# Layer 3 of a convolution network on one core: where the gate's product stands among the mask products

## The chip, the core and the metric

The kernel runs on one core of a Trainium2 chip. The metric is device time of one launch in microseconds. The five engines run their own instruction streams and meet at semaphores: PE (TensorE, the matmuls; its weight loads are shown as PEld), DVE (VectorE), ACT (ScalarE), POOL (GpSimd) and SP (SyncE); POOL and SP issue the transfers here. PE writes into PSUM, [...]and DVE and ACT read it from there.

## The reference, cut to what matters

Four layers, each a group norm and a convolution block with a residual, on x of 4 images, 48 channels, 256 x 256 pixels, all fp32. The change is in the last one:

```
y = einsum('oc,bchw->bohw', w_in, gn(x))              # 48 -> 288 channels
f = rfft2(y in 8x8 patches) * fft_mask                # one mask per channel
y = depthwise_conv3x3(irfft2(f))                      # across patch borders
x1, x2 = split(y, 2, axis=1)
out = x + einsum('oc,bchw->bohw', w_out, gelu(x1) * x2)
```

## The kernel before, in words

Layers 0 to 2 come first (about the first 11,240 us); layer 3 runs from there to the end. Its 288 channels are done in two passes of 144, the first from about 11,310 to 13,858 us and the second to 15,960 us. A pass has 64 jobs (4 images by 16 row blocks of 16 rows); a job is a row block in patches of 8 x 8, held as 64 Fourier coefficients per patch. The 128 jobs are software-pipelined in `layer3`: one turn of its last loop is a "step", and in step s the stages work on different jobs:

- `stage_a`, `stage_b` (pass 1 only) turn the normalised input of the next job into its spectrum xf and store it; in pass 2 `load_xf` (L1201, SP) reads it back in four pieces.
- `stage_c`, called as c(0) to c(7), for the current job: 8 matmuls (16 records, L1216) multiply the spectrum by w_in into the PSUM tile py, of which there is one (two banks); then four DVE products with the mask (L1228, "mask products", a pair for v=0 and a pair for v=1) write z in SBUF. c(i+1) overwrites py, so its first matmul waits for all four.
- `edges` e1 and e0 compute the border pixels of the patches (L1253), ACT copies them (L1254), and SP stores them to HBM (L1257); `above_below` and `sides` read neighbours' borders back into rows 64 to 99 of z with POOL transfers (L1266 to L1272).
- `stage_v`, called as v(0) to v(11), for the job two steps back: v(i) is half t = i % 2 of channel group g = i // 2. 12 matmuls (24 records, L1288) do inverse transform and 3x3 convolution at once into pg. An even v is followed by a gelu on ACT (L1299, into gall), an odd v by the gate's product on DVE (L1301, gall times pg). pg of even and of odd v are one bank each, with a single buffer: v(5) cannot start before the product of v(3) has read its bank, nor v(11) before that of v(9).
- `stage_t`, `last_out`, `add_out` for the job three steps back: transposes (L1309), the output matmuls (L1334), the addition to xo on DVE (L1347) and the store on SP (L1350); `load_out` (L1323, POOL) loads xo.

The order of work is written out by hand at the end of the loop and kept as it stands, engine by engine. The part in question, one step's second half:

```
            c(4), e0(0), e0(1), e0(2)
            if jv:
                load_out(jv)
            if jb:
                above_below(jb, 1)
            a(1), v(2), norm(2)
            c(5), v(3), b(1), v(4, 5)
            c(6), v(6), a(2), v(7), norm(3), v(8)
            c(7), v(9), b(2), v(10), a(3), v(11), norm(4)
```

On PE, c(5) is followed by v(3), v(4), v(5) in pass 2, where a() and the matmuls of b() are absent. In the next step come c(0), e1, the transposes, c(1), the output matmuls, c(2), more transposes, and then v(0), v(1): the first that need the border rows of z that `above_below(jb, 1)` loaded.

Of the kernel before, what the change touches and what calls it, by code (L numbers as in the profile page):

```python
# [1090 lines left out]
def layer3(k):  # L1091
# [11 lines left out]
    with ExitStack() as ctx:  # L1103
# [48 lines left out]
        def load_x(j, st):  # L1152

            for hf in range(2):
                r0 = j.u * RU + 8 * st
                nc.sync.dma_start(
                    xin[st][hf * HP : hf * HP + C], k.x3[j.b][:, r0 : r0 + 8, hf * 128 : (hf + 1) * 128]
                )

        def normalise(j, q):  # L1160
            xn = sp.tile([P112, 8, 8, 8], F32, name="xn")
            nc.scalar.activation(
                xn.rearrange("p k r w -> p r k w"),
                xin[q // 2][:, :, q % 2 * 64 : q % 2 * 64 + 64].rearrange("p r (k w) -> p r k w", w=8),
                AF.Identity,
                bias=ab3[:, j.b, 1:2],
                scale=ab3[:, j.b, 0:1],
            )
            j.x = xn.rearrange("p (k v) r w -> p k (v r w)", v=2)

        def stage_a(j):

            pt = bank()
            for i in range(4):
                nc.tensor.transpose(pt[:, i * P112 : (i + 1) * P112], j.x[:, i, :], k.ident[:P112, :P112])
            j.xt = sp.tile([128, 4, P112], F32, name="xt")
            nc.scalar.copy(j.xt.rearrange("p i c -> p (i c)"), pt[:, : 4 * P112])
# [25 lines left out]
        def columns(z):  # L1203

            return z[:, 2 : 2 + 2 * ZW].rearrange("p (s c n e) -> p s c n e", s=2, n=ZS, e=2)

        def stage_c(j, ci):

            py = ps_c.tile([128, 2, 512], F32, name="py")
            xf = j.xf[ci // 2]  # L1210
            for ii in range(2):
                i = 2 * (ci % 2) + ii
                for v in range(2):
                    for hf in range(2):
                        p = slice(hf * HP, hf * HP + C)
                        nc.tensor.matmul(  # L1216
                            py[v * HP : (v + 1) * HP, hf, ii * PASS : (ii + 1) * PASS],
                            xf[p, i, v, :],
                            wi[p, j.ps, :],
                            start=True,  # L1220
                            stop=True,
                        )
            for v in range(2):
                p = slice(v * HP, v * HP + HP)
                for hf in range(2):
                    n = hf * NPC // 2 + 4 * (ci % 4)
                    out = columns(j.z[0:64])[:, ci // 4, :, n : n + 4].rearrange("p c (i v) e -> p c i v e", v=2)
                    nc.vector.tensor_tensor(  # L1228
                        out[:, :, :, v, :],
                        py[p, hf, : 2 * PASS].rearrange("p (i c e) -> p c i e", i=2, e=2),  # L1230
                        meff[p, j.ps].rearrange("p (c e) -> p c e", e=2)[:, :, None, :].broadcast_to(
                            [HP, PASS // 2, 2, 2]
                        ),
                        ALU.mult,
                    )

# [38 lines left out]
        def load_k(j, g):  # L1277
            t = k.k3[g] = kp.tile([KZ, 4 * GP, 64], F32, name=f"kw{g}")
            nc.sync.dma_start(t.rearrange("p j x -> p (j x)"), k.kw[j.ps, g])

        def stage_v(j, g, t):


            z = columns(j.z)[..., :NPC, :]
            pg = ps_g.tile([128, GP, 2, NPC], F32, name=f"pg{t}", padded_shape=[128, 8, 2, NPC])
            for kk in range(GP):
                for e in range(2):
                    nc.tensor.matmul(  # L1288
                        pg[e * HP : (e + 1) * HP, kk],
                        k.k3[g][:, (t * GP + kk) * 2 + e, :],  # L1290
                        z[:, :, t * NP2 + g * GP + kk, :, e],
                        start=True,
                        stop=True,
                    )
            o = gall[:, g * GP : (g + 1) * GP]
            o = bass.AP(tensor=o.tensor, offset=o.offset, ap=[o.ap[0], [HP * NPC, 2], [NPC, GP], [1, NPC]])
            pg = pg.rearrange("p k s n -> p s k n")
            if t == 0:
                nc.scalar.activation(o, pg, AF.Gelu)  # L1299
            else:  # L1300
                nc.vector.tensor_tensor(o, o, pg, ALU.mult)  # L1301

        def stage_t(j, q):

            pt = [bank() for e in range(2)]
            for m in range(8):
                for e in range(2):
                    p = slice(e * HP, (e + 1) * HP)
                    nc.tensor.transpose(  # L1309
                        pt[e][: HP + NP2, m * 64 : (m + 1) * 64], gall[p, :, 8 * q + m], k.ident[p, p]  # L1310
                    )
            j.gt[q] = sp.tile([HP + NP2, 2, 512], F32, name="gt", bufs=2)
            for e in range(2):
                nc.scalar.copy(j.gt[q][:, e], pt[e][: HP + NP2])
# [10 lines left out]
        def last_out(j, h):  # L1325

            po = [bank() for st in range(2)]
            for qq in range(2):
                for e in range(2):
                    for cc in range(2):  # L1330
                        for st in range(2):
                            p = slice(st * HP, st * HP + NP2)
                            n = (HP, C)[cc]
                            nc.tensor.matmul(  # L1334
                                po[st][cc * HP : cc * HP + n, qq * 256 : (qq + 1) * 256],
                                wo[p, j.ps, e, :n],
                                j.gt[2 * h + qq][p, e, :].rearrange("p (m q x) -> p q m x", q=2, x=32)[:, cc],
                                start=(e == 0),
                                stop=(e == 1),
                            )  # L1340
            j.po = po
# [33 lines left out]
        for s in range(len(jobs) + 3):  # L1375
            jp, jc, jb, jv, jt = job(s + 1), job(s), job(s - 1), job(s - 2), job(s - 3)
            def a(q):
                if jp and not jp.ps:
                    stage_a(jp)

            def norm(q):

                nxt = jp if q < 4 else job(s + 2)
                if nxt and not nxt.ps:
                    normalise(nxt, q % 4)
                    after = job(nxt.at + 1)
                    if q % 2 and after and not after.ps:
                        load_x(after, q // 2)

            def b(q):  # L1390
                j = jp if q < 3 else jc
                if j:
                    (load_xf if j.ps else stage_b)(j, q)

            def c(i):
                if jc:
                    stage_c(jc, i)

            def t(i):
                if jt:  # L1400
                    stage_t(jt, i)

            def o(q):
                if jt:
                    last_out(jt, q)

            def v(*parts):
                for i in parts if jv else ():
                    stage_v(jv, i // 2, i % 2)
                    nxt = job(jv.at + 1)  # L1410
                    if i % 2 and nxt and nxt.ps != jv.ps:
                        load_k(nxt, i // 2)

            def e1(h):
                if jb:
                    edges(jb, 1, h)

            def e0(h):
                if jc:
                    edges(jc, 0, h)  # L1420

            def add(h):
                if jt:
                    add_out(jt, h)

            if jc:
                jc.z = zs[jc.at % 3]
            c(0), e1(0), t(0), e1(1), t(1), e1(2)
            if jb:
                above_below(jb, 0)  # L1430
                sides(jb)
            c(1), o(0), add(0), b(3)
            c(2), t(2), a(0), t(3), norm(1), v(0, 1)
            c(3), o(1), add(1), b(0)
# [3 lines that stand above are left out]
            if jb:  # L1438
                above_below(jb, 1)
            a(1), v(2), norm(2)  # L1440
            c(5), v(3), b(1), v(4, 5)
            c(6), v(6), a(2), v(7), norm(3), v(8)
            c(7), v(9), b(2), v(10), a(3), v(11), norm(4)

# [3 lines left out]
def network(ctx: ExitStack, tc: tile.TileContext, a):  # L1450
# [36 lines left out]
    layer1(k)  # L1487
    layer2(k)
    layer3(k)


# [150 lines left out]
```

## Time and profile before

| | |
|---|---|
| median of three runs | 16065.99 us (16065.2 to 16119.82) |
| the profiled execution: its time / its span | 16076.35 us / 16074.6 us |
| mean granted TensorE clock in it | 0.929 |
| mask products, L1228 | 4096 of 450 ns |
| gate's products, L1301 | 768 of 554 ns |
| gate matmuls, L1288 | 36864 records, 217 to 370 ns |
| gelus, L1299 | 768 of 492 ns |

The page's first part gives each engine's busy time; its second part cuts the span into 40 slices of 402 us, in which layer 3 has the last twelve. "PEclk" is the TensorE clock that was granted, in tenths of full speed. In the list of waits a row such as "PE pg L1288 <- DVE gall L1301" says that PE stood idle before a matmul of line 1288 until DVE finished an instruction of line 1301; the numbers are the sum in us, how often, and the longest. "issue" is idle time for which the profile shows no wait. In a timeline, equal instructions in a row are merged: start, length, engine, line, operation, count, and in brackets the idle time before them.

### The profile page before, as it was taken

The numbers are of one execution on the slowest core, as the hardware profiler recorded it, in microseconds if no ns is written. First come the engines' busy times: TensorE is split into PE (matmuls) and PEld (weight loads), VectorE is DVE, ScalarE is ACT, GpSimd is POOL, SyncE is SP. The second block draws the span as 40 slices with busy tenths as digits, with TensorE's granted clock in tenths as the row PEclk, the third lists the DMA queues.
The fourth block names the chain that finished last, engine by engine and source line by source line (L and its number), as shares of the span: only waits on it lengthen the run. The fifth ranks groups of instructions, "written<-read, shape, count | busy, mean of one in ns | idle before, by whom it ended". The sixth has DMA issues, their size and how long they took to land.

```text
span 16074.6 us, 464532 instructions
## 1 busy us (share of the span) xinstructions
PE 14620.7 (91%) x206010; PEld 10189.7 (63%) x206010; DVE 7278.4 (45%) x17024; ACT 5817.9 (36%) x11327; POOL 3452.9 (21%) x3593
## 2 busy tenths in 40 slices
PE   2988898988999999899999999998899999899998
PEld 1888884336676767555555555555666666666666
DVE  4000003333333546566666666665444444555555
ACT  1222221114432310455555555554444444323222
POOL 0000000000000036454545454544111111111111
PEclk9999999999999999999999999999778788888888
DMA  7565558998766689332322222222777777777877
GB/s 181 114 117 112 113 114 125 142 134 131 138 146 142 152 187 228 45 38 34 37 34 37 35 37 35 36 35 32 144 138 148 145 144 145 155 155 156 160 153 147
DMA packets 1998550, 1807.51 MB, mean 112 GB/s; under 512 B 1476444, under 2 KB 1755873, under 8 KB 1959489
## 3 DMA queue, kind: packets, MB, share of 16 engines
q1 hardware_dynamic: 1931002, 1501.81, 48.9%
q0 software_dynamic: 65536, 275.97, 11.0%
q8 instruction: 1617, 26.49, 0.8%
q14 instruction: 395, 3.24, 0.1%
HBM read 967.67 MB, written 625.68 MB: 99 GB/s over the span
## 4 chain that ended last, share of the span: by engine, by line
PE 80%; DMA 6%; DVE 6%; issue 4%; SPq 2%; ACT 1%; POOL 0%; DVEq 0%; POOLq 0%; ACTq 0%
PE pc L817 16%; PE p L468 14%; PE pg L1288 8%; PE ps_qk L277 7%; PE ps_o L369 5%; PE py L1216 4%; PE pm L1253 4%; PE pm L1334 3%; PE pa L848 3%; PE pm L1309 2%; PE pb L873 2%; PE gram L260 2%; PE ps_qk L281 2%; PE pb L918 2%; PE pb L927 2%
## 5 line engine op out<-in xcount | busy, mean ns | idle before, releaser
L817 PE MATMUL pc<-wg,t 50*64 50x288 f32 x49152 | 3374.9, 406 | 151.8 <-DVE qkv L833 112.5
L817 PEld LDWEIGHTS pc<-wg,t 50*64 50x64 f32 x49152 | 2013.2, 133 | 1458.3 <-issue 317.9
L1228 DVE TENSOR_TENSOR z<-py,meff 64x288 f32<-64x288 f32 x4096 | 1686.4, 450 | 1186.0 <-PE py L1216 1162.5
L1288 PE MATMUL pg<-z,kw 100*64 100x64 f32 x36864 | 1599.7, 248 | 227.5 <-issue 121.8
L1288 PEld LDWEIGHTS pg<-z,kw 100*64 100x64 f32 x36864 | 1438.8, 158 | 460.3 <-issue 275.7
L277 PE MATMUL ps_qk<-wa,ta 108*64 108x96 f32 x24576 | 1444.5, 253 | 156.1 <-issue 124.5
L468 PE MATMUL p<-carry,wk_down 96*96 96x256 f32 x6120 | 1353.3, 383 | 94.3 <-DVE carry L473 56.7
L911 POOL TENSOR_TENSOR z<-z,gb 128x768 f32<-128x768 f32 x512 | 933.1, 1822 | 2098.6 <-ACT z L905 1582.1
L277 PEld LDWEIGHTS ps_qk<-wa,ta 108*64 108x64 f32 x24576 | 1222.6, 142 | 197.7 <-issue 181.8
L833 DVE TENSOR_TENSOR qkv<-pc,c 128x576 f32<-128x576 f32 x1024 | 772.5, 754 | 1232.0 <-ACT c L832 1211.1
L468 PEld LDWEIGHTS p<-carry,wk_down 96*96 96x96 f32 x6120 | 1007.6, 165 | 439.6 <-DVE carry L473 70.1
L369 PE MATMUL ps_o<-xn,wc 48*64 48x512 f32 x9216 | 1038.9, 607 | 67.7 <-issue 49.8
L636 POOL TENSOR_TENSOR x1in<-carry,x1in 96x256 f32<-96x256 f32 x512 | 433.7, 854 | 2410.4 <-DMA x1in<-x 2215.5
L1216 PE MATMUL py<-wi,xf 48*64 48x144 f32 x16384 | 875.8, 332 | 67.8 <-issue 37.0
L840 DVE TENSOR_TENSOR qkv<-pc,qkv 128x576 f32<-128x576 f32 x1024 | 773.0, 755 | 338.7 <-PE pc L817 310.3
L1301 DVE TENSOR_TENSOR gall<-gall,pg 128x384 f32<-128x384 f32 x768 | 425.5, 554 | 1067.8 <-PE pg L1288 838.6
L369 PEld LDWEIGHTS ps_o<-xn,wc 48*64 48x64 f32 x9216 | 392.6, 137 | 713.3 <-issue 683.1
L283 ACT COPY qk<-ps_qk 128x384 f32<-128x384 f32 x512 | 244.5, 478 | 1630.2 <-PE ps_qk L281 1630.2
L281 PE MATMUL ps_qk<-wb,tb 108*64 108x96 f32 x8192 | 751.8, 253 | 84.0 <-issue 55.0
L1299 ACT ACTIVATE gall<-pg 128x384 f32<-128x384 f32 x768 | 377.5, 492 | 1043.3 <-PE pg L1288 1040.4
L173 DVE COPY g<-gram 96x96 f32<-96x96 f32 x4 | 1.0, 254 | 1657.1 <-PE gram L260 1657.1
L1216 PEld LDWEIGHTS py<-wi,xf 48*64 48x64 f32 x16384 | 564.3, 152 | 292.2 <-issue 163.9
(161 smaller groups left out, 20931.0 us busy)
## 6 DMA issues: line engine op xcount, KB each, us to landing
eb<-yb SPq DMA_DIRECT2D x1024, 148.5 KB
z<-eb POOLq DMA_DIRECT2D x512, 297.0 KB, 10.4
xf<-xf SPq DMA_DIRECT2D x512, 224.0 KB
tb<-ta SPq DMA_DIRECT2D x192, 576.0 KB
ta<-ta SPq DMA_DIRECT2D x64, 864.0 KB
xr<-x SPq DMA_DIRECT2D x120, 432.0 KB
xt<-in_x SPq DMA_DIRECT2D x32, 1536.0 KB
res<-in_x SPq DMA_DIRECT2D x64, 768.0 KB
```

The lines of the kernel that those rows point to most:

```text
L277: nc.tensor.matmul(o, ta[:, rr + dy, cols], wa[:, dy, :], start=(dy == 0), stop=False)
L281: nc.tensor.matmul(o, tb[:, rr, cols], wb, start=False, stop=True)
L369: nc.tensor.matmul(ps[cp_ * HP : (cp_ + 1) * HP, hf, :], wc[p, t, :], xn[p, r : r + 2, t % 3 : t % 3 + W], start=(t == 0), stop=(t == 8),)
L468: nc.tensor.matmul(pv, wk[name][:, o, :], old[:, :, o : o + N], start=(o == 0), stop=(o == 2))
L817: nc.tensor.matmul(pc[cc * HP : (cc + 1) * HP, h, :O], j.t[p, which, n, w0 : w0 + HP], wg[p, which, dx], start=(dx == 0), stop=(dx == 2),)
L833: nc.vector.tensor_tensor(j.qkv[:, g // 2, :, g % 2], j.pc[1][:, 0:1, :O].broadcast_to([128, 2, O]), c2, ALU.add)
L840: nc.vector.tensor_tensor(o, j.pc[0][:, :, :O], o, ALU.add)
L911: nc.gpsimd.tensor_tensor(z, z, gb[:, i : i + 1, :].broadcast_to([128, 8, Q]), op)
L1216: nc.tensor.matmul(py[v * HP : (v + 1) * HP, hf, ii * PASS : (ii + 1) * PASS], xf[p, i, v, :], wi[p, j.ps, :], start=True, stop=True,)
L1228: nc.vector.tensor_tensor(out[:, :, :, v, :], py[p, hf, : 2 * PASS].rearrange("p (i c e) -> p c i e", i=2, e=2), meff[p, j.ps].rearrange(" ...
L1253: nc.tensor.matmul(pb[32 * q : 32 * q + 32, :n], mb, z[:, a : a + n], start=True, stop=True)
L1288: nc.tensor.matmul(pg[e * HP : (e + 1) * HP, kk], k.k3[g][:, (t * GP + kk) * 2 + e, :], z[:, :, t * NP2 + g * GP + kk, :, e], start=True, ...
```

## The change

The four mask products of `stage_c` become two calls of an inner function `mask(v)`; `stage_c` issues the first and returns the second. `c(i, ...)` issues the v parts that it is given between the two. It is given v(3) with c(5) and v(9) with c(7), which stood right behind them before; all other c have nothing between.

```diff
-            for v in range(2):
+            def mask(v):
                 p = slice(v * HP, v * HP + HP)
                 for hf in range(2):
...
                         ALU.mult,
                     )
+
+            mask(0)
+            return lambda: mask(1)
...
-            def c(i):
-                if jc:
-                    stage_c(jc, i)
+            def c(i, *between):
+
+                rest = stage_c(jc, i) if jc else None
+                v(*between)
+                if rest:
+                    rest()
...
             a(1), v(2), norm(2)
-            c(5), v(3), b(1), v(4, 5)
+            c(5, 3), b(1), v(4, 5)
             c(6), v(6), a(2), v(7), norm(3), v(8)
-            c(7), v(9), b(2), v(10), a(3), v(11), norm(4)
+            c(7, 9), b(2), v(10), a(3), v(11), norm(4)
```

The order on PE, ACT, POOL and SP stays as it was. On DVE, twice a step, mask, mask, mask, mask, product becomes mask, mask, product, mask, mask. In the last turns, where there is no current job, c(5, 3) and c(7, 9) issue their v part alone.

## The prediction

> **What bounds the kernel now.** I read the page first, then the two passes of layer 3 as stretches of their own, then PE's waits in pass 2, then the timeline of a step.
>
> ```profile
> PE 14620.7 (91%) x206010; PEld 10189.7 (63%) x206010; DVE 7278.4 (45%) x17024; ACT 5817.9 (36%) x11327; POOL 3452.9 (21%) x3593
> PEclk9999999999999999999999999999778788888888
> DMA  7565558998766689332322222222777777777877
> ```
>
> PE is the engine that is nearly always busy; DVE is not near its limit. In the last twelve slices, which are layer 3, the granted clock is no longer full and the DMA engines are at 0.7 to 0.8.
>
> ```profile
> PE pg L1288 <- DVE gall L1301: 75.5, 102, 0.8
> PE pg L1288 <- issue: 51.6, 39, 4.3
> PE pg L1288 <- DMA z<-eb: 24.3, 12, 4.9
> PE pm L1309 <- DVE xo L1347: 16.6, 18, 3.7
> ```
>
> These are PE's waits in pass 2 (13,858 to 15,960 us). The first row is what the change aims at: 102 waits of 0.74 us (over the whole trace 78.5 us in 106). The same list for pass 1 has no such row: there the transforms of b(1) and of b(2) and a(3) lie between the product and v(5) or v(11), and cover it. The third row will matter too. One place in the timeline, PE and then DVE:
>
> ```profile
> 14042.82 0.72 PE L1216 MATMUL py<-wi,xf 48*64 48x144 f32 x16
> 14043.48 1.71 PE L1288 MATMUL pg<-z,kw 100*64 100x64 f32 x48
> 14045.92 0.95 PE L1288 MATMUL pg<-z,kw 100*64 100x64 f32 x24 [0.73 <-DVE gall L1301]
> 14046.80 0.46 PE L1216 MATMUL py<-wi,xf 48*64 48x144 f32 x5
> ...
> 14043.61 1.66 DVE L1228 TENSOR_TENSOR z<-py,meff 64x288 f32<-64x288 f32 x4 [1.66 <-PE py L1216]
> 14045.31 0.56 DVE L1301 TENSOR_TENSOR gall<-gall,pg 128x384 f32<-128x384 f32 x1
> 14046.99 0.56 DVE L1301 TENSOR_TENSOR gall<-gall,pg 128x384 f32<-128x384 f32 x1 [1.12 <-PE pg L1288]
> ```
>
> c(5) at 42.82 (I drop the 14,000), v(3) and v(4) from 43.48, v(5) at 45.92, c(6) at 46.80. DVE does four masks to 45.27, then the product of v(3) to 45.87; 0.05 us later v(5) starts.
>
> **The change at one place, full clock, pass 2.** Nothing is added or removed: as many DVE instructions, of the same durations, in another order; no transfer is moved, and no queue but DVE's is reordered. The first pair of masks ends at 43.61 + 1.66/2 = 44.44. The product then waits for PE: where DVE stands free, the product of v(5) starts 46.99 - 45.92 = 1.07 us after that v's first matmul, so that of v(3) starts at 43.48 + 1.07 = 44.55 (DVE idles 0.11 us, with the second mask pair behind it) and ends at 45.11. Its other input, the gelu of v(2), ended at 43.44 and doesn't delay it. v(5) can start at 45.16; v(4)'s matmuls are issued until about 45.0, so the wait all but vanishes: 45.92 - 45.16 = 0.76 us sooner.
>
> What is late next? The second pair ends at 45.13 + 0.83 = 45.96, 0.7 us later than before, and c(6) must wait for it because py is single. c(6) would come at 46.80 - 0.76 = 46.04, py is free at about 46.01. So that cover is just enough; if it fails by a tenth, the price is 0.1 us x 106 = 11 us. Edges don't feel the later masks: z of c(5) and c(7) is first read by e1 of the next step.
>
> So at most 106 x 0.75 = 80 us lie here. At half clock nothing is to be had: the product is released by slower matmuls, and v(5) and v(11) show no wait on it. In pass 1 the second pair also ends 0.7 us later, but c(6) and c(0) come 4.0 us or more after their predecessors at full clock, well behind it; I put pass 1 at nothing (bounds: 4 us gained, where v(5) is barely covered, 5 lost).
>
> **Where the saved time goes.** Both places lie between e0, which starts the chain of border transfers, and v(0) of the next step, which needs them. Here is a step in which v(0) came to wait:
>
> ```profile
> 14943.22 0.57 POOL L1323 DMA_DIRECT2D xo<-y  x1 [10.86 <-DVE z L1228]
> 14948.74 0.51 POOL L1266 DMA_DIRECT2D z<-eb  x1 [4.05 <-DMA eb<-yb]
> 14949.75 0.51 POOL L1268 DMA_DIRECT2D z<-eb  x1
> ...
> 14955.37 1.62 PE L1309 MATMUL pm<-ident,gall 64*100 64x64 f32 x32
> 14959.47 2.83 PE L1288 MATMUL pg<-z,kw 100*64 100x64 f32 x48 [2.48 <-DMA z<-eb]
> ```
>
> The borders are stored by SP, read by POOL at 948.74 to 949.75, and land some 9 us later. PE got there 2.48 us early although it had lost 1.48 us at v(5) and v(11). I compared, job by job in pass 2, the last landing of z<-eb with the first matmul of v(0): in 27 of 60 jobs v(0) starts within 0.55 us of it. From c(4), a full-clock step needs 24.2 us to v(0) without such a wait, and the landing comes after 22 to 28 us, median 25.8. Where the landing is last, PE saves 1.5 us earlier and waits 1.5 us longer at v(0). Summing for each step the smaller of its slack there and its two stalls gives 34.9 of 68.4 us in 58 steps; scaled to the 78.5 us, **40 us**; with the occasional py wait, about 35.
>
> **The clock.** These stretches are a clean step, a step held by the landing but at full clock, and the two steps around the wait of 2.48 us (columns: length, busy time of PE, PEld, DVE, ACT, POOL, granted clock, DMA share, GB/s):
>
> ```profile
> 14345.02:14373.35 28.33, 26.65 (x592) 19.42 (x593) 18.84 (x43) 9.77 (x20) 4.73 (x9) 1.00 0.80 164
> 14535.92:14566.42 30.50, 27.29 (x592) 19.92 (x593) 18.91 (x43) 9.86 (x20) 5.10 (x10) 1.00 0.82 164
> 14932.62:14966.66 34.04, 29.97 (x592) 22.00 (x596) 18.86 (x42) 9.86 (x20) 5.34 (x10) 0.89 0.86 164
> 14966.66:15000.07 33.41, 32.48 (x597) 22.94 (x589) 18.89 (x43) 9.76 (x20) 5.34 (x10) 0.81 0.77 144
> 14959.00:14979.50 20.50, 20.03 (x264) 14.12 (x264) 7.80 (x17) 2.94 (x6) 5.34 (x10) 0.50 0.81 156
> ```
>
> The wait was followed by 20.5 us at half clock. The two steps took 67.45 us against 2 x 30.50 = 61: a price of 6.5 us. Pass 2 has 38 such drops, 519 us at half clock in all. About 15 begin around v(0), mostly for 17 to 24 us, where z or xo is late; waits of z above 2.1 us nearly all brought one, waits about 1 us mostly not. Ten begin within 5 us behind one of the waits that the change removes (106 us at half clock, so some 53 us lost, since a half-clock us costs about half a us), most of them with an "issue" gap as well.
>
> The Trainium skill speaks to this ("TensorE: Matmul & The Clock Gate", section on the HAM clock gate): the clock halves after an idle window of about 3.4 us. By that rule moving 1.5 us into a wait of 1 us costs no clock, and only the 35 us count. By the row above 2.48 us sufficed. The trace decides: I expect more long drops at v(0), about four more at 6.5 us (26 us), and about half of the ten others gone (26 us). These cancel, and neither can be sized better than to a factor of two.
>
> **The sum.** 16076.35 - 35 = 16041 in the profiled execution's own terms; that one was 10 us above the median, so from the median 16066 - 35 = **16031 us**.
>
> **The rivals.**
> - *The gain comes in full, and the clock helps* (chance 0.22). The denser PE stream loses the ten drops: -80 and up to -53 more, net of landings between 15,935 and 15,990, say 15,975. For it: landing times follow e0, which follows PE, so the chain is earlier too in later steps. Against it: 27 of 60 jobs have no slack now.
> - *The wait just moves* (0.20). The DMA share of 0.80 to 0.86 in full-clock steps means the transfers set the pace of every run of fast steps; slack after a slow step is used up sooner. Gain 5 us: 16,060. The same time would follow if the second pair were late for c(6) by as much as the product is early. That the order is not carried out is unlikely: in the timeline above DVE does exactly the written order.
> - *More half clock* (0.14). At v(0) of pass 2, waits of 1 us become 2.5 us, and the clock halves for 20 us at 6.5 us a time. It beats the 35 us from six net added drops on, and needs 18 to be slower by 0.5% (115/6.5). Fourteen steps now wait 0.4 to 1.5 us there without much harm; with twelve more, +43: 16,109. Against it: each drop gives the transfers time to catch up (after one, slack is 9 to 14 us), so drops prevent one another.
>
> The partial gain, 16,031, keeps 0.44. I call "same" what is within 0.5%, or 80 us, about what a measurement of this kernel can tell from no change. Faster (below 15,986) takes most of the first rival and a little of the main case, 0.20; slower (above 16,146) takes the larger part of the last, 0.10; same 0.70. The range goes from the full gain without much of the clock's help, 15,945, to more half clock, 16,115.
>
> **What would show it.** In the changed profile the row "pg <- gall" on PE should fall from 75 us to under 10 in pass 2 (the step of the product); c(6) should come 3.2 us after c(5) in place of 4.0, with little or no wait of py on the masks; waits of v(0) on z<-eb, 24 us now, should double (the step of the landing); half clock in pass 2 should stay near 519 us. If it moves by more than 150 us either way, the clock has decided, and my cancelling was wrong; if the z waits stay as they are, the full gain should be there; pass 1 should keep its 2,548 us.

## The result, and the profile after

The changed kernel takes 16085.24 us (median of 14 runs, 16031.29 to 16119.74) against 16071.19 us of 14 runs of the kernel before. The ratio worked out from all of these runs is 1.0004, 95% interval 0.999 to 1.0017. That is no change that can be measured, and the 35 us of gain that the prediction named as likeliest lie outside the interval. The profiled execution took 16058.56 us, with a span of 16056.8 us. One execution of the seventh experiment below, of 22,851 us, was far slower than all its like and is left out there.

The same three rows of the page, after (the changed kernel's lines have other numbers: L1217 is L1216 of before, L1230 is L1228, L1293 is L1288, L1306 is L1301):

```profile
PE 14671.9 (91%) x206010; PEld 10254.8 (64%) x206010; DVE 7280.5 (45%) x17024; ACT 5819.9 (36%) x11327; POOL 3453.0 (22%) x3593
PEclk9999999999999999999999999999788877888888
DMA  8565658998766679322222222222677777777877
```

PE shows 51 us more busy time for the same 206010 matmuls: they ran at a lower clock (0.925 in the mean, 0.929 before). PE's waits in pass 2, after:

```profile
PE pg L1293 <- issue: 47.4, 41, 3.2
PE pm L1314 <- issue: 18.4, 12, 3.8
PE pg L1293 <- DMA z<-eb: 16.9, 15, 2.3
PE pm L1314 <- DVE xo L1352: 16.6, 21, 2.7
...
PE pg L1293 <- DVE gall L1306: 0.3, 1, 0.3
```

The wait that the change aims at went from 75.5 us to 0.3 us. The waits for the border transfers, which were to double, fell from 24.3 to 16.9 us. The timeline of one place, PE and then DVE (c(5), then v(3) to v(5) in one run, then c(6)):

```profile
14665.10 0.72 PE L1217 MATMUL py<-wi,xf 48*64 48x144 f32 x16
14665.75 2.64 PE L1293 MATMUL pg<-z,kw 100*64 100x64 f32 x72
14668.32 0.72 PE L1217 MATMUL py<-wi,xf 48*64 48x144 f32 x16
...
14665.89 0.81 DVE L1230 TENSOR_TENSOR z<-py,meff 64x288 f32<-64x288 f32 x2 [1.65 <-PE py L1217]
14666.83 0.55 DVE L1306 TENSOR_TENSOR gall<-gall,pg 128x384 f32<-128x384 f32 x1
14667.41 0.84 DVE L1230 TENSOR_TENSOR z<-py,meff 64x288 f32<-64x288 f32 x2
```

c(6) comes 3.22 us after c(5) (3.98 before), and its py is free in time: the second mask pair ends at 68.25, c(6) starts at 68.32. So the place does what was worked out. Here is pass 2 as a whole, from c(0) of its first job to c(0) of its last, before and then after:

```profile
13871.36:15972.28 2100.92, 1898.67 (x37301) 1370.21 (x37297) 1189.93 (x2646) 621.01 (x1260) 337.07 (x631) 0.88 0.79 157
```

```profile
13862.76:15954.27 2091.51, 1948.23 (x37300) 1397.35 (x37297) 1189.67 (x2646) 622.65 (x1260) 338.52 (x633) 0.85 0.79 158
```

The length hardly moved, and the granted clock fell from 0.88 to 0.85. The first two numbers of each row show where the time went: PE's idle time, length less busy time, fell by 59 us (202 to 143), and the same matmuls took 50 us longer (1898.67 to 1948.23). The trace's record of the clock has only full and half: in pass 2, 519 us at half before and 628 us after. If a us at half clock counts as half a us of work, pass 2 is 2100.9 - 259 = 1841 us at full clock before and 2091.5 - 314 = 1777 after: by this estimate 64 us were freed, and 55 given back through the clock. By stretches of a step (from each c to the next, means in us over 60 steps of pass 2, counted from the trace):

| from | c(0) | c(1) | c(2) | c(3) | c(4) | c(5) | c(6) | c(7) |
|---|---|---|---|---|---|---|---|---|
| length before | 5.21 | 3.13 | 5.48 | 2.92 | 4.23 | 4.36 | 3.54 | 4.49 |
| length after | 5.61 | 3.43 | 5.57 | 3.01 | 4.40 | 3.77 | 3.58 | 3.74 |
| at half clock before | 1.05 | 0.80 | 2.15 | 0.86 | 1.23 | 0.98 | 0.64 | 0.48 |
| at half clock after | 1.19 | 1.50 | 2.51 | 1.08 | 1.56 | 1.16 | 0.37 | 0.35 |
| clock drops begun before / after | 2 / 12 | 5 / 7 | 15 / 14 | 0 / 0 | 0 / 0 | 4 / 0 | 2 / 3 | 8 / 4 |

1.34 us a step are gained behind c(5) and c(7), and 1.05 lost from c(0) to c(4). A "drop" is a change from full to half clock; 38 begin in pass 2 before and 43 after. Those behind c(5) to c(7) are halved (14 to 7); ten new ones begin behind c(0).

**What "issue" is.** Waits without a visible cause are 72 us of PE's waits in pass 2 before, against 120 for all others, and 95 us after, against 38. I compared the 46 of them above 0.7 us in pass 2 after (84.9 us; before 38 with 61.8 us) with the DMA packets of the queue of kind "instruction": these are 16,384 bytes each, and 8 in 10 of the waits end 1.31 to 1.95 us after the end of such a packet, where 8 in 10 instants drawn at random lie 0.7 to 8.2 us after one. They stand mostly at multiples of 256 PE instructions, matmuls and weight loads together, from one another. So PE waits for its own code ("late code" below), and it does so less when there is less data to move (the fifth experiment) and more when the transfers are bunched (the third). The Trainium skill ("Runtime: NRT & Kernel Launch", "Instruction fetch mechanics") has the blocks of 16 KiB and calls the cost of going from one to the next mostly hidden; here 85 us aren't. One such wait, PE's timeline and then the stretch behind it (columns as in the prediction):

```profile
14684.17 1.53 PE L1314 MATMUL pm<-ident,gall 64*100 64x64 f32 x30 [0.67 <-issue]
14688.54 2.79 PE L1293 MATMUL pg<-z,kw 100*64 100x64 f32 x48 [2.85 <-issue]
```

```profile
14688.60:14692.10 3.50, 3.50 (x64) 3.38 (x68) 0.56 (x1) 0.49 (x1) 2.25 (x5) 0.51 0.52 100
```

After 2.85 us without code the clock is at half.

### The profile page after: what moved, and what is told of

The parts are those of the page before. It is cut to its first block, busy times and chain, and to the rows that moved or that the text cites. A ratio compares the mean times of both kernels' runs of the same rounds, so it can differ in the third digit from the quotient of the medians.

```text
span 16056.8 us, 464660 instructions
## 1 busy us (share of the span) xinstructions
PE 14671.9 (91%) x206010; PEld 10254.8 (64%) x206010; DVE 7280.5 (45%) x17024; ACT 5819.9 (36%) x11327; POOL 3453.0 (22%) x3593
## 4 chain that ended last, share of the span: by engine, by line
PE 80%; DMA 6%; DVE 6%; issue 5%; SPq 1%; ACT 1%; POOL 0%; DVEq 0%; POOLq 0%; ACTq 0%
PE pc L817 15%; PE p L468 15%; PE pg L1293 9%; PE ps_qk L277 7%; PE ps_o L369 6%; PE py L1217 4%; PE pm L1258 4%; PE pm L1339 3%; PE pa L848 3%; PE gram L260 3%; PE pb L873 2%; PE pm L1314 2%; PE ps_qk L281 2%; PE pb L918 2%; PE pb L927 2%
## 5 line engine op out<-in xcount | busy, mean ns | idle before, releaser
L1230 DVE TENSOR_TENSOR z<-py,meff 64x288 f32<-64x288 f32 x4096 | 1684.9, 450 | 1227.8 <-PE py L1217 1199.3
L1293 PE MATMUL pg<-z,kw 100*64 100x64 f32 x36864 | 1592.0, 248 | 139.7 <-issue 120.0
L1293 PEld LDWEIGHTS pg<-z,kw 100*64 100x64 f32 x36864 | 1433.7, 158 | 369.5 <-issue 260.4
L1217 PE MATMUL py<-wi,xf 48*64 48x144 f32 x16384 | 884.3, 336 | 68.8 <-issue 40.3
L1306 DVE TENSOR_TENSOR gall<-gall,pg 128x384 f32<-128x384 f32 x768 | 425.6, 554 | 970.5 <-PE pg L1293 725.0
L369 PEld LDWEIGHTS ps_o<-xn,wc 48*64 48x64 f32 x9216 | 432.0, 138 | 676.1 <-issue 628.2
L1217 PEld LDWEIGHTS py<-wi,xf 48*64 48x64 f32 x16384 | 572.2, 154 | 297.4 <-issue 175.5
L1258 PE MATMUL pm<-z,mb 64*32 64x396 f32 x6144 | 737.6, 581 | 15.5 <-issue 14.3
```

Source lines behind the costliest of these rows:

```text
L369: nc.tensor.matmul(ps[cp_ * HP : (cp_ + 1) * HP, hf, :], wc[p, t, :], xn[p, r : r + 2, t % 3 : t % 3 + W], start=(t == 0), stop=(t == 8),)
L1217: nc.tensor.matmul(py[v * HP : (v + 1) * HP, hf, ii * PASS : (ii + 1) * PASS], xf[p, i, v, :], wi[p, j.ps, :], start=True, stop=True,)
L1230: nc.vector.tensor_tensor(out[:, :, :, v, :], py[p, hf, : 2 * PASS].rearrange("p (i c e) -> p c i e", i=2, e=2), meff[p, j.ps].rearrange(" ...
L1258: nc.tensor.matmul(pb[32 * q : 32 * q + 32, :n], mb, z[:, a : a + n], start=True, stop=True)
L1293: nc.tensor.matmul(pg[e * HP : (e + 1) * HP, kk], k.k3[g][:, (t * GP + kk) * 2 + e, :], z[:, :, t * NP2 + g * GP + kk, :, e], start=True, ...
```

## The experiments

Each experiment edits either the kernel before ("old order") or the changed one ("new order"), and two kernels that differ by the order alone are twins. Theories. *Clock*: PE's freed time arrives, and more half-clock time takes it back. *Landing*: the border transfers set the step, and the wait moves there. *Load*, a form of the first: late code and late data, both from busy DMA engines, open the gaps that halve the clock. The rivals were that the two places differ, or that a denser PE stream is slowed whatever the transfers do.

**1 and 2. One place at a time.** With c(5) alone:

```diff
-            c(7, 9), b(2), v(10), a(3), v(11), norm(4)
+            c(7), v(9), b(2), v(10), a(3), v(11), norm(4)
```

> The change at c(5) alone, c(7) and v(9) as before. Clock theory (the removed waits of PE arrive in full as time at full clock, and more time at half clock takes them back): PE's wait of the gate matmuls on the gate's product falls from 75 to about 38 us in pass 2, pass 2 less half of its half-clock time falls by some 30 us (from 1841), its half-clock time lies above the 519 us of before, and the time is within 25 us of before. Landing theory (the transfers of borders set the step, whatever the clock): waits of v(0) on them rise by some 15 us and the time stays; half clock unchanged. If the two places act differently: this one alone faster by 30 us or more.

And c(7) alone:

```diff
-            c(5, 3), b(1), v(4, 5)
+            c(5), v(3), b(1), v(4, 5)
```

> The change at c(7) alone, c(5) and v(3) as before. Clock theory: as with the first place alone, wait on the product about 38 us, time within 25 us of before, half clock above 519 us in pass 2. Landing theory: waits of v(0) on the borders up by 15 us, time unchanged, half clock unchanged. If the two places act differently: one of them alone is faster by 30 us and the other slower by as much.

16096.9 and 16095.87 us: ratios to before 1.0013 (1.0002 to 1.0024) and 1.0013 (1.0001 to 1.0025), so if anything a little slower than before. The wait on the product fell to 42.6 and 32.5 us. Pass 2 at full clock, reckoned as above, was 1817 and 1803 us, half clock 577 and 604 us. Half the change frees about half the time and loses it to the clock too; no difference between the places can be measured.

**3 and 4. Borders that are never late.**

```diff
-            rows = k.eb[j.b % 2][1 - st].rearrange("b r n -> (b r) n")
+            rows = k.eb[(j.b + j.ps) % 2][1 - st].rearrange("b r n -> (b r) n")
...
                 above_below(jb, 0)
                 sides(jb)
+                if jb.ps:
+                    above_below(jb, 1)
...
-            if jb:
+            if jb and not jb.ps:
                 above_below(jb, 1)
```

(In `sides` the buffer is chosen likewise.)

> Order of before. In pass 2 the border rows are read from the buffer of the neighbouring image and all at the early place, so that as many bytes are moved but no landing is late; the borders are thus not the reference's in pass 2. Landing theory: the waits of v(0) on borders vanish (24 us), with them most drops of the clock at v(0): 80 to 150 us faster than before. Clock theory (drops come from any idle of PE, those without a visible wait too): 30 to 80 us faster, half clock in pass 2 still above 350 us.

> The change, with the border rows in pass 2 read from the neighbouring image's buffer and all at the early place (the borders are not the reference's in pass 2). Against the same with the order of before. Landing theory: the change now pays, 60 to 80 us faster than its twin. Clock theory: again within 25 us of its twin, and with more half-clock time than it by 80 us or more.

Both theories were wrong on the third kernel: 16361.6 us, a ratio of 1.018 (1.0157 to 1.0204). No v(0) waited for borders any more; PE's largest waits in pass 2 were these:

```profile
PE pm L1334 <- issue: 83.7, 15, 8.7
PE py L1216 <- issue: 80.6, 16, 7.3
PE pg L1288 <- DVE gall L1301: 79.4, 108, 0.8
PE pm L1253 <- issue: 57.5, 12, 8.7
...
PE pg L1288 <- issue: 37.8, 19, 9.1
```

The same bytes, asked for in one burst behind c(0), kept the code away for up to 9.1 us at a time, 306 us in all; half clock rose to 910 us. This is what led to the reading of "issue" above. With the change (16393.46 us, 1.0198, 1.0169 to 1.0226) the result is as for the clock theory: 69 us less in the product of time and clock (see the table below), no gain in time, and half clock of 1079 us. Since the edit also bunched the transfers, it does not tell what borders in time would be worth by themselves.

**5 and 6. Fewer transfers.**

```diff
-            if jb:
+            if jb and not jb.ps:
                 above_below(jb, 0)
                 sides(jb)
...
-            if jb:
+            if jb and not jb.ps:
                 above_below(jb, 1)
```

> Order of before; in pass 2 the border rows are not read back at all (133 of 322 MB of the pass's transfers left out, and the borders are not the reference's). Load theory (late landings and late code, both from the load on the DMA engines, open the idle gaps of PE that halve the clock): the gaps without a visible wait fall below half of the 62 us of before, half clock in pass 2 below 250 us, and the kernel is 150 to 230 us faster than before. Rival (the clock follows PE's own pattern of work and not the transfers): half clock stays above 400 us and it is less than 80 us faster.

> The change, with the border rows not read back in pass 2 (left out as in its twin, the borders are not the reference's). Load theory: the 75 us now arrive, 60 to 90 us faster than its twin with the order of before. Rival (a denser PE stream is slowed by the clock whatever the transfers do): within 25 us of its twin, with 80 us or more of added half clock.

The "133 MB" were mistaken: that is all of POOL's traffic, xo's loads included. What is left out is some 85 MB (157 GB/s over 2100.9 us against 130 over 1884.5). The fifth kernel took 15826.63 us, a ratio of 0.984 (0.9813 to 0.9866); late code fell from 61.8 to 22.8 us, half clock to 181 us. That is more gain than the 150 to 230 us that were expected, and it says that the transfers' load makes most of pass 2's late code and drops. Pass 2 of the two, old order and then new:

```profile
13870.44:15754.90 1884.46, 1757.82 (x37300) 1265.51 (x37297) 1187.86 (x2646) 618.81 (x1260) 75.80 (x137) 0.95 0.53 130
```

```profile
13906.73:15718.40 1811.67, 1757.00 (x37300) 1266.50 (x37297) 1187.91 (x2646) 619.46 (x1260) 76.24 (x137) 0.95 0.55 135
```

At equal clock the change is worth 72.8 us in pass 2 of these profiles, nearly all of it. But the sixth kernel's median, 15806.87 us, is only 20 us below its twin's (means: 22 us, +-14), where the load theory had 60 to 90: a miss. In its profile layers 0 to 2, which are the same, took 29 us longer, and its mean clock over the runs was lower (0.9355 against 0.9396). Where in those runs the clock was lost, one profile each can't tell.

**7. The stall doubled.**

```diff
+                again = 2 if j.ps and v and ci in (5, 7) else 0
-                for hf in range(2):
+                for hf in [0, 1] + [1] * again:
```

> Order of before, but in pass 2 the last mask product of c(5) and of c(7) is issued three times instead of once, so that the gate's product and with it v(5) and v(11) come 0.83 us later: each of the two waits grows from 0.74 to about 1.57 us, some 88 us in all. Clock theory (what PE waits there is lost elsewhere if it isn't waited there): pass 2 less half of its half clock rises by 60 to 90 us, half clock falls below 519 us, and the time rises by less than 40 us. Rival (the waits lie on the path at full price, and the change failed for a cost of its own): the time rises by 75 to 95 us.

16266.45 us, a ratio of 1.0111 (1.0084 to 1.0139): more than either theory gave it. PE's timeline at one of the lengthened waits, and the stretches behind it and then ahead of it:

```profile
14482.62 1.70 PE L1289 MATMUL pg<-z,kw 100*64 100x64 f32 x48
14486.05 1.14 PE L1289 MATMUL pg<-z,kw 100*64 100x64 f32 x24 [1.73 <-DVE gall L1302]
```

```profile
14486.60:14513.90 27.30, 26.70 (x366) 18.84 (x364) 12.58 (x28) 6.21 (x13) 4.76 (x9) 0.50 0.69 139
14464.70:14482.60 17.90, 17.68 (x346) 11.37 (x344) 11.66 (x26) 7.82 (x16) 2.69 (x5) 1.00 0.59 104
```

A wait of 1.73 us brought 27 us of half clock; of the 66 drops in those 60 steps 36 begin behind c(5) or c(6) and 25 behind c(0), just behind the two lengthened waits (6 and 2 before). Half clock in pass 2 rose to 1021 us, where the clock theory had it fall. So the clock does not give back elsewhere what is waited here: a wait of 0.75 us at this place is mostly harmless to it, one of 1.73 us is not.

The traces say more on that. In each of them all drops of pass 2 lie on one grid of 3.41 us. I took every window of this grid in pass 2 that ran at full clock, in all 14 traces, and summed PE's idle time in it (gaps above 0.2 us):

| idle in the window, us | 0 to 0.8 | 0.8 to 1.5 | above 1.5 |
|---|---|---|---|
| windows | 5465 | 374 | 395 |
| a drop at its end | 18 | 164 | 395 |

The waits that the change removes are of the harmless kind: windows with 0.6 to 0.8 us of idle fell from 80 to 11 in pass 2, and only one of the 80 ended in a drop. Those above 1.5 us stayed (26 and 27).

**8 to 10. Loads moved out of the busy stretch.** Before, the DMA engines are 0.92 to 0.99 busy behind c(3) and c(4), 0.94 behind c(6) and c(7), and 0.57 to 0.59 behind c(1) and c(2), so two loads of xf were moved:

```diff
-                if j:
+                if j and j.ps and q == 3:
+                    load_xf(j, 2)
+                if j and not (j.ps and q in (1, 2)):
...
             c(7), v(9), b(2), v(10), a(3), v(11), norm(4)
+            if jp and jp.ps:
+                load_xf(jp, 1)
```

For the eighth, c() issues its second pair ahead of the v part in pass 1.

> The change in pass 2 alone (pass 1 keeps the four masks together), with two of the four spectrum loads of a step in pass 2 issued later, as in the next two kernels. It asks what pass 1 contributes. If the new order costs something in pass 1 by the clock, as the half-clock time of the profiles hints (about 1100 us in pass 1 with the change, about 1055 without), this kernel is 10 to 20 us faster than its twin with the new order in both passes; if pass 1 is indifferent, within 10 us of it.

> Order of before; of the spectrum loads in pass 2 the one after c(5) is issued after v(11), and the one after c(7) after c(1) of the next step, so that 448 KB of a step leave the stretch c(5) to c(7), where the DMA engines are 0.76 to 0.94 busy, for c(0) to c(2), where they are 0.57 to 0.76. Load theory: fewer gaps of late code in c(5) to c(7), half clock in pass 2 down by some 50 to 100 us, 20 to 50 us faster than before. Rival (only the order of the work on PE counts): within 15 us of before.

> The change, with the same later loads. Load theory: with the busiest stretch relieved part of the 75 us arrives: 20 to 50 us faster than its twin with the order of before, 50 to 90 us faster than before. Rival: within 15 us of its twin.

Old order: 15992.92 us, 0.9961 (0.9944 to 0.9979), the one version here with the reference's computation that is measurably faster than before. New order: 16050.15 us, 0.9994 (0.998 to 1.0009), by the means 46 us (+-25) slower than its twin: a miss of both expectations, for here the change costs more than it frees. In pass 2, old order and then new:

```profile
13839.90:15858.74 2018.84, 1842.24 (x37300) 1338.21 (x37296) 1188.85 (x2646) 620.75 (x1260) 335.91 (x628) 0.91 0.80 163
```

```profile
13846.44:15891.87 2045.43, 1893.07 (x37299) 1364.51 (x37297) 1189.61 (x2646) 621.00 (x1260) 335.38 (x627) 0.87 0.79 160
```

Late code 51.1 against 67.9 us (waits above 0.7 us, as before), waits of v(0) on borders 11 against 25 us, of c() on xf 13 against 25 us, half clock 375 against 512 us. So most of the removed wait came back as other waits, and the clock fell besides. With the change in pass 2 alone 16055.04 us, 5 us from the twin with both passes: pass 1 makes no difference that can be measured.

**11 and 12. A third load moved**, behind the border stores (against the ninth and the tenth):

```diff
-                if j and not (j.ps and q in (1, 2)):
+                if j and not (j.ps and q < 3):
...
             c(4), e0(0), e0(1), e0(2)
+            if jp and jp.ps:
+                load_xf(jp, 0)
```

> Order of before with the later loads, and in pass 2 the first spectrum load of a step too is issued later, behind the border stores of e0, which it stood ahead of on SP. If the landing of the borders at v(0) still costs, waits of v(0) on them fall from 13 us and the time falls 10 to 40 us below that of the later loads alone (which were 0.39% under before); if not, within 15 us of it.

> The change with all three loads later. If the clock takes back what the change frees as long as the transfers are this dense, it is again slower than its twin with the order of before, by 20 to 60 us, at a product of time and mean clock that is 40 to 70 us smaller. If the earlier borders were what it lacked, it is 20 us or more faster than its twin.

16074.73 us (1.0014, 0.9993 to 1.0035) and 16122.78 us (1.0042, 1.0024 to 1.006). The border waits fell to 6.7 and 3.3 us, but now xf was late: PE's largest waits in the eleventh,

```profile
PE pg L1288 <- DVE gall L1301: 86.7, 117, 0.8
PE py L1216 <- DMA xf<-xf: 47.2, 20, 21.3
```

(88.1 us in the twelfth). Again the new order loses, by 41 us (+-34), as the clock theory had it; the later xf may have as much part in it.

All pairs together, as means over the runs (the 43 are the runs of the kernel before beside the first four experiments, the 14 those of the result). The product of an execution's time and its mean clock is what it would have taken at full clock, roughly, if nothing but PE's work were stretched by a slow clock and all of it by two:

| | old order: time, clock, product | new order: time, clock, product |
|---|---|---|
| as they are (43 and 14 runs) | 16077.5, 0.9269, 14903 | 16077.5, 0.9238, 14852 |
| one place (22 runs each) | | 16098 and 16095, 0.924, 14877 both |
| early borders | 16366.6, 0.9175, 15016 | 16392.2, 0.9118, 14947 |
| no borders | 15827.1, 0.9396, 14871 | 15805.3, 0.9355, 14786 |
| two loads later | 15999.5, 0.9322, 14914 | 16045.2, 0.9258, 14854 |
| three loads later | 16087.0, 0.9264, 14903 | 16128.4, 0.9211, 14856 |

The new order lowers the product by 47 to 85 us in every pair, each product with a standard error of 3 to 8 us, and the clock each time by 0.003 to 0.006. Only with fewer transfers is anything left of it. A lower product alone doesn't show that time was freed, though: the seventh kernel, which adds a stall, has 14878 against 14908 of the runs of before beside it; at its lower clock PE waited less for code (19 us of "issue" in pass 2 against 72). PE's idle and busy time in pass 2 need no such reckoning. New less old order, one profile each, in us:

| | wait on the product | all idle time | the same matmuls | length |
|---|---|---|---|---|
| as they are | -75 | -59 | +50 | -9 |
| early borders | -79 | -16 | +52 | +36 |
| no borders | -81 | -72 | -1 | -73 |
| two loads later | -78 | -24 | +51 | +27 |
| three loads later | -85 | -20 | +105 | +85 |

As the kernels are, most of the removed wait stays away, and slower matmuls take it. In three other pairs most of it comes back as other waits, and the matmuls get slower as well.

## Why the prediction was right, and where it wasn't

- *The place.* Right in each term: 0.76 us sooner, product 1.07 us behind v(3)'s first matmul (66.83 - 65.75 = 1.08 us), py free just in time.
- *What the change frees.* "35 us" was too small: 59 us of idle time are gone from pass 2, and by the estimates at full clock 64 us of pass 2 and 51 us of the whole.
- *The landing.* The step that failed. The stalls removed at v(5) and v(11) did not come back as waits of v(0): 24.3 us became 16.9, and the jobs without slack 27 became 24 of 60. The slack was summed as if every landing stood still, but the stores that start the chain follow PE, as the first rival said, and the slack that a slow step gives back was counted nowhere. Its sign "if the z waits stay as they are, the full gain should be there" failed too: they fell, and the time stayed. (The "DMA share of 0.80 to 0.86 in full-clock steps" is a misreading of the rows: 0.86 is the share of a step with a mean clock of 0.89; at full clock the rows have 0.80 and 0.82.)
- *The clock.* "These cancel" was wrong in its parts. The drops behind v(5) and v(11) fell by half as expected (14 to 7 from c(5) to c(7)), those at v(0) stayed (15 and 14), and ten came behind c(0), which the prediction did not have. Half clock rose by 109 us, some 55 us of time, less than the 150 us that were to tell of the clock, and this loss stands where the landing's was put. That the clock takes the gain is the third rival, "more half clock", in another place than it named.
- *"issue".* The row was shown and only counted as a companion of drops; it is late code. It rose by 23 us in pass 2, and the prediction had no term for it.
- *The time.* The range and "no measurable change" held by luck, because a loss of about the right size stood in another place than named; the likeliest 35 us did not come. The rival "the wait just moves", at 16,060, had the better time, but the gain went to the clock, not to the landing.
- *Pass 1* is indifferent, as put: from its first c(0) to that of pass 2 it took 2587.6 us before and 2580.6 after.

Shown: that as the kernels are PE's idle time falls and its matmuls slow by about as much, the lower clock in all pairs, that the load of transfers makes most of the late code and of the drops (fifth kernel), and that bunching them makes more (third). Argued only: why the new drops begin behind c(0). Code runs late there in 11 steps after against 4 before (waits above 0.4 us, 20.5 against 3.4 us), just behind a stretch in which the DMA engines are 0.94 busy and which PE now leaves 1.3 us sooner. Open: why only some 20 of the 73 us arrive in the sixth kernel's time.

## What to carry to other kernels

Where the clock follows gaps, a stall's price is not its length: here a wait of 0.75 us alone cost hardly any clock, and one of 1.7 us could cost tens of us at half clock. So compare idle time, busy time and granted clock of a stage before and after, and not the waits alone. Waits marked "issue" can be late code, which competes with the data's transfers; here moving two loads out of a busy stretch was worth more than the order of two vector instructions. Test a schedule edit again with the next bottleneck eased, for it may lose there too.

## What the runs showed of the hardware

- The clock halved at the end of every window of 3.41 us with more than 1.5 us of idle time in PE (395 of 395), and of hardly any with less than 0.8 us (18 of 5465). The Trainium skill ("TensorE: Matmul & The Clock Gate", Part 1, which the prediction weighed) has the clock at half after an idle window of about 3.4 us: the length agrees with the grid of the traces, but the window need not be idle as a whole. The half clock then lasted 3.4 to 34 us in pass 2 before and after, in multiples of 3.4 us.
- PE waited for its code up to 9.1 us when a burst of border transfers stood ahead.
- Bringing the border rows earlier in one burst, with the same bytes, made the kernel 1.8% slower; bringing two of a step's four spectrum loads later made it 0.4% faster, and a third one later undid that.
